# Weight products of layer 2's attention computed beside the Mamba scans of layer 0 and kept in DRAM

## The chip, the cores and the metric

The kernel runs on one core of one Trainium2 chip. The metric is the time of one execution on the device, in microseconds (us); the lower, the better. All tensors are 32-bit floats except where a name says otherwise. Engines are named as the profile names them: PE (matmuls; PEld its weight loads), DVE (vector), ACT (scalar), POOL (GpSimd), SP (here it only issues DMAs).

## The reference, cut to what matters

An image of 2 x 256 x 48 x 48 goes through four layers: layer 0 is a bidirectional Mamba block, layer 1 a linear attention with a convolution and an MLP, layer 2 a "split attention" and a mixture of experts with graph routing, layer 3 an attention with sigmoid and a second mixture of experts. The change concerns layer 2's attention, with three heads on tokens `x` (2304 per image, 256 channels):

```python
def head(W, b):                       # W: 768 x 256, b: 768
    e = einsum('bmc,hc->bmh', x, W) + b
    q, k, v = split(e, 3, axis=1)     # by thirds of the TOKENS, not of the features
    attn = softmax(einsum('bmd,bnd->bmn', q, k) * 256**-0.5)
    return einsum('bmn,bnd->bmd', attn, v)
outs = vmap(head)(W_embed, b_embed)   # three heads
out = einsum('bmd,cd->bmc', concat(outs, axis=1), W_out) + b_out + x
```

Since all three thirds use one matrix `W`, the kernel never forms `e`. The scores are `x_q (WᵀW) x_kᵀ` up to terms that the softmax removes, and the value path is `attn x_v (Wᵀ W_outᵀ)`. So the kernel needs, for each head, the 256 x 512 matrix `Wᵀ [W | W_outᵀ]`, called `gm`, and two vectors of 256, `Wᵀb` and `W_out b + b_out`, called `ub`. Both depend on weights alone.

Layer 0's scan is the recurrence `h = exp(dt·A) h + (dt·u) B`, `y = Σ_n h_n C_n`, for 512 channels, 16 states `n`, 2304 positions, 2 images and 2 directions.

## The kernel before

**Layer 0** (`layer0`) cuts a sequence into 6 chunks of `W = 384` positions. `order` lists 24 scans: image 0 forward (0 to 5), image 0 backward (6 to 11), image 1 forward (12 to 17), image 1 backward (18 to 23). One call of `scan` goes over 4 blocks of 128 channels in two pairs and 16 states in groups of 4. In a group, SP loads `bb` and `cc` (rows of B and C spread over the partitions, 768 KB each) into double buffers, POOL makes `db` (L332), and for each state ACT computes the exponential `hs` into a PSUM bank (L346), DVE runs the recurrence (L352 forward, L355 backward), DVE or POOL multiplies by C into `hc` (L360, five buffers), and PE adds `hc` into the PSUM tile `yp` by an identity matmul (L363).

Other work is woven into a scan as generators: after every second state, `slot` (1 to 32 in a scan) goes up and each entry of `beside` advances in proportion to its numbers (steps, slots by which they are to be done). These entries are `project_out` of the scan before (2 steps, only after a backward scan), `prepare` of the next scan (15 steps), and `project_in` of a later chunk (12 steps; scans 0 to 9 have one, scans 10 to 23 none). All three take their PSUM tile from `hold()`, which during the scans is the pool `ps` with the tag "mm": one bank, one buffer. The eight banks are five for `hs`, one for "mm", two for `yp`. `project_in` has ten such tiles, `prepare` nine, `project_out` two. ACT reads most of them out; DVE reads out both of `project_out` (L314) and the first of `project_in`.

The order on each engine's queue is set when the program is built, by a scheduler that starts from the order of the code and lets work that it reckons ready go first. The profile shows this: at the start of layer 2, DVE instructions of `sort_rest` (L862 to L881) and of `normalize_piece` (L95 to L105) alternate.

**Layer 1 to layer 2.** The last MLP chunk of layer 1 ends with L617 to L625 (DVE), and the last `normalize_piece` (PE L95 and L101, DVE L96, L104, L105, ACT L98, L103) makes the last 384 columns of the normalized tokens `xn`. Then `sort_rest` sorts what was left of the edge lists, on DVE. `layer2_attn` begins with the weight products: for each head, two DMAs bring `w_eo` (W_embed of the head and W_outT, 768 KB each, L675 and L676, two buffers), PE makes `gm` in two pieces of 512 columns over 6 blocks of rows (L680) and the columns of `ub` (L688), and DVE copies them out (L684, L692, L693). Then the attention proper runs for image 0 and image 1: transposes of `xn` (L708, copied out by DVE L709), `qq` = gm·xn (L717, ACT L721), scores (L729), softmax (DVE L734, ACT L738), and so on.

Of the kernel before, what the change touches and what calls it, by code (L numbers as in the profile page):

```python
# [5 lines left out]


# [1 line left out]

# [1 line left out]

# [20 lines left out]
W = 384  # L32
# [19 lines left out]
class Env:  # L52


    def __init__(self, ctx, tc, p):
        nc = self.nc = tc.nc
        self.tc, self.p, self.n_pools = tc, p, 0
        const = ctx.enter_context(tc.tile_pool(name="const", bufs=1))
        self.const = const
        self.dram = ctx.enter_context(tc.tile_pool(name="dram", bufs=1, space=DRAM))  # L60
        self.vec = const.tile([P, _NV], F32, name="vec")
        nc.sync.dma_start(self.vec, p["vecs"])
        self.ident = const.tile([P, P], F32, name="ident")
        make_identity(nc, self.ident)
        self.mean_c = const.tile([P, P], F32, name="mean_c")
        nc.vector.memset(self.mean_c, 1.0 / C)
        self.eps = {}
        for e in (1e-5, 1e-6):
            t = const.tile([P, 1], F32, name=f"eps{len(self.eps)}")
            nc.vector.memset(t, e)  # L70
            self.eps[e] = t
        self.xres = const.tile([P, 2, T], F32, name="xres")

    def uid(self):
        self.n_pools += 1
# [41 lines left out]
def layer0(ctx, E):  # L117
# [8 lines left out]
    nc, tc, p = E.nc, E.tc, E.p  # L126
# [22 lines left out]
    def hold():  # L149

        pool, tag = (ps, "mm") if scanning else (psh, "hs")
        return pool.tile([P, W], F32, tag=tag, name="mm")

    def project_in(b, c):

# [148 lines left out]
    def project_out(b, c, y):  # L304

        for m in range(2):
# [7 lines left out]
            nc.vector.tensor_tensor(xr, xr, po, ALU.add)  # L314
            yield

    def scan(step, beside, b, s, c, xs, y, dt, dtu, bcd):

        fwd = s == "f"
        yp = [None] * DB  # L320
        if not fwd:
            yf = up.tile([P, DB, W], F32, tag="ln", name="yf")
            nc.sync.dma_start(yf, yf_d[b][:, c])
        slot, done = 0, [0] * len(beside)
        for d0, g in [(d0, g) for d0 in range(0, DB, 2) for g in range(NS // GN)]:
            bb = wp.tile([P, GN, W], F32, tag="bb", name="bb")
            nc.sync.dma_start(bb, bcd[16 + g * GN : 16 + (g + 1) * GN, :].partition_broadcast(P))
            cc = wp.tile([P, GN, W], F32, tag="cc", name="cc")
            nc.sync.dma_start(cc, bcd[32 + g * GN : 32 + (g + 1) * GN, :].partition_broadcast(P))
            for d in (d0, d0 + 1):  # L330
                db = wp.tile([P, GN, W], F32, tag="db", name="db")
                nc.gpsimd.tensor_tensor(db, bc(dtu[:, d, :], [P, GN, W], 1), bb, ALU.mult)  # L332
                if g == 0:
                    yp[d] = psy.tile([P, W], F32, tag=f"y{d % 2}", name=f"yp{d}")
                    nc.tensor.matmul(
                        yp[d], lhsT=w_d[s][:, d, :], rhs=xs[:, d, :], start=True, stop=False
                    )
                    if not fwd:
                        nc.tensor.matmul(
                            yp[d], lhsT=E.ident, rhs=yf[:, d, :], start=False, stop=False  # L340
                        )
                for j in range(GN):
                    n = g * GN + j
                    on_pool = j in GP[(g + d) % 2]
                    hs = psh.tile([P, W], F32, tag="hs", name="hs")
                    nc.scalar.activation(  # L346
                        hs, dt[:, d, :], AF.Exp, scale=nega[s][:, d * NS + n : d * NS + n + 1]
                    )
                    to = wp.tile([P, W], F32, tag="ho", name="ho") if on_pool else hs
                    init = 0.0 if step == 0 else state[:, d, n : n + 1]  # L350
                    if fwd:
                        nc.vector.tensor_tensor_scan(to, hs, db[:, j], init, ALU.mult, ALU.add)  # L352
                        last = to[:, W - 1 : W]
                    else:
                        nc.vector.tensor_tensor_scan(  # L355
                            to[:, ::-1], hs[:, ::-1], db[:, j, ::-1], init, ALU.mult, ALU.add
                        )
                        last = to[:, 0:1]
                    hc = wp.tile([P, W], F32, tag="hc", name="hc", bufs=5)
                    (nc.gpsimd if on_pool else nc.vector).tensor_tensor(hc, to, cc[:, j, :], ALU.mult)  # L360
                    if step < NCH - 1:
# [12 lines left out]
        if fwd:  # L374
            nc.sync.dma_start(yf_d[b][:, c], y)
        for steps, _, _ in beside:
            for _ in steps:
                pass
# [10 lines left out]
    scanning = True  # L389
    pieces = [(0, c) for c in range(2, NCH)] + [(1, c) for c in range(NCH)]  # L390
    after = None
    for i, (b, s, step, c) in enumerate(order):
        now, ready = ready, []
        beside = [(after, 2, 5)] if after else []
        if i + 1 < len(order):
            nb, s2, _, c2 = order[i + 1]
            beside.append((prepare(nb, s2, c2, ready), 15, 25))
        if i < len(pieces):
            beside.append((project_in(*pieces[i]), 12, 32))
        scan(step, beside, *now)  # L400
        after = project_out(b, c, now[4]) if s == "b" else None
    for _ in after:
# [251 lines left out]
def layer2_attn(ctx, E):  # L654

    nc, tc, p = E.nc, E.tc, E.p
    NH, D = 3, 768  # L660
    S = L // NH
    DT, ST, HW2 = D // P, S // P, S // 2
    scale = C**-0.5
    big = ctx.enter_context(tc.tile_pool(name="l2big", bufs=1))
    xn = E.xn
    gm = big.tile([P, NH, 2, 2 * C], F32, name="gm")
    ub = big.tile([P, NH, 4], F32, name="ub")
    with (
        tc.tile_pool(name="l2wt", bufs=2) as wts,
        tc.tile_pool(name="l2wps", bufs=2, space=PSUM) as ps,  # L670
    ):
        for h in range(NH):

            w_eo = wts.tile([P, DT, 2 * C], F32, tag="w_eo", name="w_eo")
            nc.sync.dma_start(w_eo[:, :, 0:C], p["W_embed"][h].rearrange("(k p) m -> p k m", p=P))  # L675
            nc.sync.dma_start(w_eo[:, :, C:], p["W_outT"].rearrange("(k p) m -> p k m", p=P))  # L676
            for m in range(2):
                pg = ps.tile([P, 2 * C], F32, tag="pg", name="pg")
                for k in range(DT):
                    nc.tensor.matmul(  # L680
                        pg, lhsT=w_eo[:, k, m * P : (m + 1) * P], rhs=w_eo[:, k, :],
                        start=k == 0, stop=k == DT - 1,
                    )
                nc.vector.tensor_copy(gm[:, h, m, :], pg)  # L684
            pu = ps.tile([P, 4], F32, tag="pu", name="pu")
            for m in range(4):
                for k in range(DT):
                    nc.tensor.matmul(  # L688
                        pu[:, m : m + 1], lhsT=w_eo[:, k, m * P : (m + 1) * P],
                        rhs=E.v("b_embed", h * DT + k, 1), start=k == 0, stop=k == DT - 1,  # L690
                    )
            nc.vector.tensor_copy(ub[:, h, 0:2], pu[:, 0:2])  # L692
            nc.vector.tensor_tensor(ub[:, h, 2:4], pu[:, 2:4], E.v("b_out"), ALU.add)  # L693

    act = ctx.enter_context(tc.tile_pool(name="l2act", bufs=2))
    wp = ctx.enter_context(tc.tile_pool(name="l2w", bufs=2))
# [4 lines left out]
    for b in range(NB):  # L701
        t0 = b * L
        xv = act.tile([P, ST, C], F32, tag="xv", name="xv", bufs=1)
        for t in range(ST):
            o = t0 + 2 * S + t * P
# [4 lines left out]
        for h in range(NH):  # L710
            qq = act.tile([P, 2, S], F32, tag="qq", name="qq")
            for m in range(2):
                for g in range(2):
                    gs = slice(g * HW2, (g + 1) * HW2)
                    pq = ps.tile([P, HW2], F32, tag="mm", name="pq")
                    for k in range(2):
# [1 line left out]
                            pq, lhsT=gm[:, h, k, m * P : (m + 1) * P],  # L718
                            rhs=xn[:, k, t0 + g * HW2 : t0 + (g + 1) * HW2], start=k == 0, stop=k == 1,
                        )  # L720
                    nc.scalar.activation(qq[:, m, gs], pq, AF.Identity, bias=ub[:, h, m : m + 1])  # L721

            pT = act.tile([P, ST, S], F32, tag="pT", name="pT", bufs=1)
            for t in range(ST):
# [39 lines left out]
            for m in range(2):  # L764
                for g in range(2):
                    o = t0 + h * S + g * HW2
                    py = ps.tile([P, HW2], F32, tag="mm", name="py")
                    for k in range(2):
# [3 lines left out]
                        )  # L772
                    y = wp.tile([P, HW2], F32, tag="y", name="y")
                    nc.vector.scalar_tensor_tensor(
                        y, py, ub[:, h, 2 + m : 3 + m], xn[:, m, o : o + HW2], ALU.add, ALU.add
                    )
                    xr = E.xres[:, m, o : o + HW2]
                    nc.gpsimd.tensor_tensor(xr, xr, y, ALU.add)
# [1087 lines left out]
```

## Time and profile before

| | us |
|---|---|
| median of 3 runs | 5647.52 (5646.13 to 5651.45) |
| the profiled execution, whole | 5647.58 |
| its span, first to last instruction | 5645.4 |
| PE busy | 4877.7 (86%) |
| DVE busy | 3527.2 (62%) |
| POOL busy | 2398.8 (42%) |
| ACT busy | 2368.0 (42%) |
| scans of layer 0, first to last L352/L355 | 111.7 to about 2494 |
| weight products of layer 2 on PE | 3220.9 to 3275.0 |

The whole execution is 2.2 us longer than the span. The page also cuts the span into 40 slices of about 141 us with each engine's busy share. A group of instructions is given as "line, engine, operation, out<-in, shapes, count | busy us, mean ns of one | idle time before them and what ended it". A PE matmul of 32-bit floats shows as two records, so a count of 72 is 36 matmuls of the code.

### The profile page before, as it was taken

Reading aid. Unit: us, or ns where it says so; the run is one execution under the profiler, and the core shown is the slowest. Engines: PE = TensorE matmul, PEld = TensorE weight load, DVE = VectorE, ACT = ScalarE, POOL = GpSimd, SP = SyncE. Lnnn points to the kernel's source line nnn. Section 1 sums busy time; section 2 is a strip of 40 time slices with the busy share of each in tenths; the row PEclk is TensorE's granted clock in tenths of the full one; section 3 lists DMA queues with packets and bytes.
Section 4 is the critical chain, followed back from the end, with each engine's and each line's share of the span. In section 5 each row is a group of like instructions: output and inputs, shape, how many; then the busy total and the mean of one; then the engine's idle time right before and its main releaser. Section 6 shows DMA issues by size and latency. Waiting matters only on the chain. (4 is left out here: it accounts for less than half of the span.)

```text
span 5645.4 us, 47582 instructions
## 1 busy us (share of the span) xinstructions
PE 4877.7 (86%) x15480; PEld 2694.9 (48%) x15480; DVE 3527.2 (62%) x5198; ACT 2368.0 (42%) x4880; POOL 2398.8 (42%) x1295
## 2 busy tenths in 40 slices
PE   7888788877777778779999999999799999997996
PEld 3444343433333333335555555566455455554664
DVE  4899978888999988899993224456524311212333
ACT  5777666655676666622222223322033222221220
POOL 3887877777898887750000000058212100000212
PEclk9999999999999899989999999999899999998997
DMA  4444444433434444330100100111011100000323
GB/s 157 162 170 165 169 148 157 148 141 135 164 150 166 159 154 149 140 128 31 41 30 2 34 5 1 42 34 27 8 57 45 45 6 9 6 9 13 87 75 78
DMA packets 173648, 486.59 MB, mean 86 GB/s; under 512 B 31488, under 2 KB 96517, under 8 KB 173125
## 3 DMA queue, kind: packets, MB, share of 16 engines
q1 hardware_dynamic: 165252, 471.82, 23.5%
q0 software_dynamic: 8128, 11.55, 1.6%
q8 instruction: 126, 2.06, 0.1%
q14 instruction: 142, 1.16, 0.1%
HBM read 416.44 MB, written 66.86 MB: 86 GB/s over the span
## 5 line engine op out<-in xcount | busy, mean ns | idle before, releaser
L363 PE MATMUL yp<-hc,ident 128*128 128x384 f32 x3072 | 1234.5, 529 | 388.8 <-POOL hc L360 295.3
L332 POOL TENSOR_TENSOR db<-dtu,bb 128x1536 f32<-128x1536 f32 x384 | 1332.2, 3470 | 153.7 <-DVE ho L355 55.1
L363 PEld LDWEIGHTS yp<-hc,ident 128*128 128x128 f32 x3072 | 579.0, 200 | 980.8 <-POOL hc L360 454.0
L360 POOL TENSOR_TENSOR hc<-ho,cc 128x384 f32<-128x384 f32 x576 | 587.6, 1029 | 153.8 <-PE yp L363 90.7
L360 DVE TENSOR_TENSOR hc<-hs,cc 128x384 f32<-128x384 f32 x960 | 498.8, 537 | 51.0 <-PE yp L363 48.8
L346 ACT ACTIVATE hs<-dt,negab 128x384 f32<-128x384 f32 x768 | 436.2, 581 | 98.6 <-DVE ho L355 54.9
L346 ACT ACTIVATE hs<-dt,negaf 128x384 f32<-128x384 f32 x768 | 433.8, 581 | 59.2 <-DVE ho L352 28.6
L355 DVE TENSOR_TENSOR_SCAN hs<-hs,state,db 128x384 f32<-128x384 f32 x400 | 393.4, 1006 | 29.3 <-ACT hs L346 20.0
L352 DVE TENSOR_TENSOR_SCAN hs<-hs,state,db 128x384 f32<-128x384 f32 x400 | 394.9, 1006 | 20.0 <-POOL db L332 14.2
L1691 POOL DMA_INDIRECT xe<-xt_d,token x48 | 49.0, 1020 | 779.9 <-issue 768.5
L1623 PE MATMUL po<-at,xtok 128*128 128x384 f32 x864 | 334.1, 508 | 7.9 <-ACT at L1621 7.9
L252 PE MATMUL mm<-xw,w_cv 128*128 128x384 f32 x768 | 290.5, 512 | 52.9 <-DVE xres L314 18.8
L879 POOL PARTITION_ALL_REDUCE most<-most x1 | 0.4, 380 | 743.9 <-DVE ub L693 743.9
L1616 PE MATMUL sp<-qT,xn 128*128 128x384 f32 x864 | 312.1, 486 | 0.0
L1320 PE MATMUL ph<-xn,w 128*128 128x384 f32 x768 | 283.0, 510 | 23.1 <-issue 7.2
L1621 ACT ACTIVATE at<-sp 128x384 f32<-128x384 f32 x216 | 104.6, 490 | 466.1 <-PE sp L1616 463.3
L355 DVE TENSOR_TENSOR_SCAN ho<-hs,state,db 128x384 f32<-128x384 f32 x240 | 239.7, 999 | 61.8 <-POOL hc L360 52.3
L1629 DVE TENSOR_TENSOR xres<-xres,po 128x384 f32<-128x384 f32 x24 | 13.3, 554 | 410.8 <-PE po L1623 409.8
L612 PE MATMUL po<-hid,wfc 128*128 128x384 f32 x768 | 256.8, 488 | 0.0
L594 PE MATMUL pf<-t,wfc 128*128 128x384 f32 x768 | 255.3, 489 | 0.0
L352 DVE TENSOR_TENSOR_SCAN ho<-hs,state,db 128x384 f32<-128x384 f32 x240 | 238.5, 994 | 8.4 <-ACT hs L346 4.4
L1324 ACT ACTIVATE hid<-ph,vec 128x384 f32<-128x384 f32 x192 | 111.1, 580 | 301.2 <-PE ph L1320 243.6
(423 smaller groups left out, 8203.8 us busy)
## 6 DMA issues: line engine op xcount, KB each, us to landing
bb<-bcd SPq DMA_DIRECT2D x192, 768.0 KB
cc<-bcd SPq DMA_DIRECT2D x192, 768.0 KB
xw<-xi_d SPq DMA_DIRECT2D x24, 774.0 KB
w<-in_m_w SPq DMA_DIRECT2D x16, 1024.0 KB
y_d<-y SPq DMA_DIRECT2D x32, 384.0 KB
ye<-y_d SPq DMA_DIRECT2D x32, 384.0 KB
xi_d<-xz SPq DMA_DIRECT2D x48, 192.0 KB
z_d<-xz SPq DMA_DIRECT2D x48, 192.0 KB
```

The costliest lines, as they stand in the source:

```text
L252: nc.tensor.matmul(px, lhsT=w_cv[b, s][:, d * 4 + k, :], rhs=xw[:, d, o : o + W], start=k == 0, stop=k == 3,)
L332: nc.gpsimd.tensor_tensor(db, bc(dtu[:, d, :], [P, GN, W], 1), bb, ALU.mult)
L346: nc.scalar.activation(hs, dt[:, d, :], AF.Exp, scale=nega[s][:, d * NS + n : d * NS + n + 1])
L352: nc.vector.tensor_tensor_scan(to, hs, db[:, j], init, ALU.mult, ALU.add)
L355: nc.vector.tensor_tensor_scan(to[:, ::-1], hs[:, ::-1], db[:, j, ::-1], init, ALU.mult, ALU.add)
L360: (nc.gpsimd if on_pool else nc.vector).tensor_tensor(hc, to, cc[:, j, :], ALU.mult)
L363: nc.tensor.matmul(yp[d], lhsT=E.ident, rhs=hc, start=False, stop=n == NS - 1)
L594: nc.tensor.matmul(pf, lhsT=wfc1[:, k, f * P : (f + 1) * P], rhs=t1[:, k, :], start=k == 0, stop=k == 1,)
L612: nc.tensor.matmul(po[m], lhsT=wfc2[:, f, m * P : (m + 1) * P], rhs=hid[:, i, :], start=f == 0, stop=f == 15,)
L1320: nc.tensor.matmul(ph, lhsT=w1[:, e, k, f * P : (f + 1) * P], rhs=xn[:, k, c * W : (c + 1) * W], start=k == 0, stop=k == 1,)
L1616: nc.tensor.matmul(sp, lhsT=xn[:, k, t0 + i * P : t0 + (i + 1) * P], rhs=qT[:, k, c * W : (c + 1) * W], start=k == 0, stop=k == 1,)
L1623: nc.tensor.matmul(po[m], lhsT=xtok[:, i, m * P : (m + 1) * P], rhs=at, start=i == 0, stop=i == MT - 1,)
```

## The change

Layer 2's block of weight products is taken out. A generator `head_products` in `layer0` computes the same numbers in 12 steps of three yields (head `h`, half `m` of the 256 rows, half `z` of the 768 rows summed over), one step in each of the scans 10 to 21. In a step, six DMAs load three blocks of `w_eo` (a block is 128 rows of 256 floats from W_embed and as many from W_outT, 128 KB each) into the buffers of the tags "pos", "h" and "sq", which `project_in` no longer needs; three matmuls of 512 columns go into a "mm" tile, six matmuls of one column into another. For `z == 0` ACT copies the first tile into `part` and DVE the second into `E.ub`; for `z == 1` DVE adds to both, and `part` is stored in the DRAM tile `gm_d`. `E.ub` stays on the chip; `gm` is loaded in layer 2 by three DMAs of 512 KB. `hold()` and `hs` ask for 512 columns and use 384 of them.

```diff
+        self.gm_d = self.dram.tile([3, 2, P, 2 * C], F32, name="gm_d")
+        self.ub = const.tile([P, 3, 2, 2], F32, name="ub")
...
         pool, tag = (ps, "mm") if scanning else (psh, "hs")
-        return pool.tile([P, W], F32, tag=tag, name="mm")
+        return pool.tile([P, 512], F32, tag=tag, name="mm")[:, :W]
...
+    def head_products():
+        DT, D = 6, 768
+        for h, m, z in [(h, m, z) for h in range(3) for m in range(2) for z in range(2)]:
+            w_eo = []
+            for k in range(3):
+                rows = slice((z * 3 + k) * P, (z * 3 + k + 1) * P)
+                t = up.tile([P, 2, W], F32, tag=("pos", "h", "sq")[k], name="w_eo")
+                t = t.rearrange("p k w -> p (k w)")[:, : 2 * C]
+                nc.sync.dma_start(t[:, 0:C], p["W_embed"][h, rows, :])
+                nc.sync.dma_start(t[:, C:], p["W_outT"][rows, :])
+                w_eo.append(t)
+            yield
+            pg = ps.tile([P, 2 * C], F32, tag="mm", name="pg")
+            for k in range(3):
+                nc.tensor.matmul(
+                    pg, lhsT=w_eo[k][:, m * P : (m + 1) * P], rhs=w_eo[k], start=k == 0, stop=k == 2
+                )
+            if z == 0:
+                part = up.tile([P, 2 * C], F32, tag="part", name="part")
+                nc.scalar.copy(part, pg)
+            else:
+                nc.vector.tensor_tensor(part, part, pg, ALU.add)
+                nc.sync.dma_start(E.gm_d[h, m], part)
+            yield
+            pu = ps.tile([P, 2 * C], F32, tag="mm", name="pu")
+            for i in range(2):
+                o = i * C + m * P
+                for k in range(3):
+                    nc.tensor.matmul(
+                        pu[:, i : i + 1], lhsT=w_eo[k][:, o : o + P],
+                        rhs=E.v("b_embed", h * DT + z * 3 + k, 1), start=k == 0, stop=k == 2,
+                    )
+            ub = E.ub[:, h, m, :]
+            if z == 0:
+                nc.vector.tensor_copy(ub, pu[:, 0:2])
+            else:
+                nc.vector.tensor_tensor(ub, ub, pu[:, 0:2], ALU.add)
+                nc.vector.tensor_tensor(ub[:, 1:2], ub[:, 1:2], E.v("b_out", m, 1), ALU.add)
+            yield
...
-                    hs = psh.tile([P, W], F32, tag="hs", name="hs")
+                    hs = psh.tile([P, 512], F32, tag="hs", name="hs")[:, :W]
...
+    heads = head_products()
     for i, (b, s, step, c) in enumerate(order):
...
         if i < len(pieces):
             beside.append((project_in(*pieces[i]), 12, 32))
+        elif i < len(pieces) + 12:
+            beside.append((islice(heads, 3), 3, 32))
...
     gm = big.tile([P, NH, 2, 2 * C], F32, name="gm")
-    ub = big.tile([P, NH, 4], F32, name="ub")
-    with (
-        tc.tile_pool(name="l2wt", bufs=2) as wts,
-        tc.tile_pool(name="l2wps", bufs=2, space=PSUM) as ps,
-    ):
-        for h in range(NH):
...
+    ub = E.ub
+    for h in range(NH):
+        nc.sync.dma_start(gm[:, h], E.gm_d[h].rearrange("m p c -> p m c"))
```

The lines left out at the end are the loop of weight products described with the kernel before; the two readers of `ub` (L721, L774) only change their index.

More of the change, by code (lines that the diff above doesn't have):

```diff
@@ L8 @@
 from contextlib import ExitStack
+from itertools import islice
 import numpy as np
@@ L659, in layer2_attn @@
     nc, tc, p = E.nc, E.tc, E.p
-    NH, D = 3, 768
+    NH = 3
     S = L // NH
-    DT, ST, HW2 = D // P, S // P, S // 2
+    ST, HW2 = S // P, S // 2
     scale = C**-0.5
@@ L666, in layer2_attn @@
     gm = big.tile([P, NH, 2, 2 * C], F32, name="gm")
-    ub = big.tile([P, NH, 4], F32, name="ub")
-    with (
-        tc.tile_pool(name="l2wt", bufs=2) as wts,
-        tc.tile_pool(name="l2wps", bufs=2, space=PSUM) as ps,
-    ):
-        for h in range(NH):
[L674 to L693, printed above, removed]
+    ub = E.ub
+    for h in range(NH):
+        nc.sync.dma_start(gm[:, h], E.gm_d[h].rearrange("m p c -> p m c"))
     act = ctx.enter_context(tc.tile_pool(name="l2act", bufs=2))
@@ L720, in layer2_attn @@
                         )
-                    nc.scalar.activation(qq[:, m, gs], pq, AF.Identity, bias=ub[:, h, m : m + 1])
+                    nc.scalar.activation(qq[:, m, gs], pq, AF.Identity, bias=ub[:, h, m, 0:1])
             pT = act.tile([P, ST, S], F32, tag="pT", name="pT", bufs=1)
@@ L774, in layer2_attn @@
                     nc.vector.scalar_tensor_tensor(
-                        y, py, ub[:, h, 2 + m : 3 + m], xn[:, m, o : o + HW2], ALU.add, ALU.add
+                        y, py, ub[:, h, m, 1:2], xn[:, m, o : o + HW2], ALU.add, ALU.add
                     )
```

## The prediction

> **What bounds the kernel now.** I read the slices first, to see which engine is full where, then the groups and the timeline at the start of layer 2, where work is taken away, then the scans one by one, where it is put. Slices of the page, 141 us each:
>
> ```profile
> PE   7888788877777778779999999999799999997996
> DVE  4899978888999988899993224456524311212333
> ```
>
> The scans fill slices 0 to 17: DVE is at 8 to 9 tenths and PE at 7 to 8. Layer 2 begins in slice 22: PE is full, DVE is not. So the change moves PE work from a stage that PE bounds into one that DVE bounds. The groups give its size:
>
> ```profile
> L680 PE MATMUL pg<-w_eo 128*128 128x512 f32 x72 | 34.3, 635 | 0.0
> L688 PE MATMUL pu<-vec,w_eo 128*128 128x1 f32 x144 | 18.0, 258 | 3.2 <-DMA w_eo<-in_W_embed 3.2
> ```
>
> Busy 34.3 and 18.0 us, and one wait of 3.2 us for the weights. The timeline says whether anything else ran meanwhile:
>
> ```profile
> 3203.51 10.48 PE L612 MATMUL po<-hid,wfc 128*128 128x384 f32 x32
> ...
> 3216.22 1.56 PE L95 MATMUL ln_mean<-xres,mean_c 128*128 128x384 f32 x4 [2.22 <-DVE xres L625]
> ...
> 3220.93 3.35 PE L688 MATMUL pu<-vec,w_eo 128*128 128x1 f32 x22 [3.15 <-DMA w_eo<-in_W_embed]
> ...
> 3224.14 2.91 PE L101 MATMUL ln_var<-ln_sq,mean_c 128*128 128x384 f32 x4
> ...
> 3275.21 2.79 PE L708 MATMUL tp<-ident,xn 128*128 128x128 f32 x12 [0.41 <-DVE ub L693]
> ```
>
> PE goes from layer 1's last matmul (ends 3213.99) to the attention's first transpose (3275.21) in 61.2 us, without a break from 3220.9. The products lie on the path that sets the end. The scans, one window each (PE, PEld, DVE, ACT, POOL busy, then clock, DMA share, GB/s):
>
> ```profile
> 399.60:498.40 98.80, 81.87 (x226) 42.47 (x225) 89.97 (x113) 70.36 (x169) 81.95 (x42) 0.95 0.44 164
> 1358.40:1458.40 100.00, 80.18 (x217) 40.36 (x216) 81.39 (x111) 63.09 (x157) 81.21 (x42) 0.95 0.39 142
> 1548.10:1637.00 88.90, 70.06 (x185) 32.96 (x185) 86.78 (x108) 62.00 (x155) 82.44 (x42) 0.96 0.43 160
> 1909.50:2005.70 96.20, 71.69 (x178) 34.63 (x178) 84.49 (x113) 59.11 (x148) 81.89 (x43) 0.86 0.40 150
> 2109.00:2209.80 100.80, 77.74 (x210) 38.67 (x209) 86.23 (x114) 65.31 (x154) 81.34 (x42) 0.93 0.40 149
> ```
>
> These are scan 3 (forward, with `project_in`), 12 (first forward scan of image 1, with `project_out`), 14 (forward, with nothing but `prepare`), 18 (first backward, no `project_out`) and 20 (backward, with `project_out`). DVE is idle for 2.1 us of scan 14, and 9 to 19 us of the others. Scans 13 to 17 are of the tight kind, and five of the twelve new steps fall into them. Why the others are loose shows in who waited for `project_out`'s read-out on DVE (L314), us and times:
>
> ```profile
>   PEld mm L252: 23.1, 7
>   PE mm L252: 18.8, 7
> ```
>
> PE stands at the next convolution's matmul (L252) until DVE has freed the single "mm" bank, and behind it stand the `hc` matmuls.
>
> **What the Trainium skill says.** "TensorE: Matmul & The Clock Gate" (Architectural detail): PE may pull weight loads ahead of matmuls in flight, while ACT and DVE work strictly in order. So a wait at one matmul holds all behind it; the two rows above agree. "Perfetto Trace Analysis" (Optimizing Scalar/DVE Operations): an operation has a fixed overhead, on PSUM for DVE about 125 ns. The trace agrees in kind: a copy of two columns (L692) took 159 ns, so small steps are paid per instruction. "PSUM — Partial Sum Buffer" (The four PSUM rules): 512 floats fill one bank; `pg` with its 512 columns fits the "mm" bank, so the padding to 512 needs no more banks if a buffer takes a bank anyway, which no row here shows. I cost it at nothing.
>
> **The change part by part.**
>
> *Layer 2.* Of the 61.2 us, the four matmuls of L95 (1.6) and those of L101 (2.9) stay: at most 56.7 are saved, if the waits of 2.2 and 3.2 us are filled too (the transposes need only tokens of image 0, long ready). If both waits stay, 51.3. New in their place: three loads of 512 KB. The stretch that loaded the old weights moved 345 GB/s in its best slice; 1.57 MB is 4.6 us, behind which only L717 waits, not the transposes. They need nothing but room in SBUF: if that comes free when it did for L675 (3215.65), the last lands near 3221, when L717 would start. I cost them at nothing to 3 us. The cover that goes: DVE's `sort_rest` and last normalization lay beside the products. The windows 3215:3221 and 3221:3245 hold 5.8 + 11.6 us of DVE; less two copies of `gm` and one pair of `ub` (1.7), plus the six L709 (2.6): 18.3 us, so DVE is free at 3233.5 at best. PE needs its first softmax maximum at 3217.8 + 2.8 (L708) + 6.7 (L717) + 2.9 (L101) + 2.6 (first scores) = 3232.8. These are level, so a loss of 0 to 12 us if L709 stands late in DVE's queue; I take 2. **Gain 49, from 39 to 57.**
>
> *Layer 0, work.* PE gets the same 72 and 144 records: at their pace in the old block (0.43 and 0.12 us) 31 + 17 = 48 us over twelve scans, 4 each. PE is idle for 19 us in scan 14 and 23 to 25 in the backward ones: covered, except for its order. ACT gets six copies of 512 columns; L193, 384 columns, takes 478 ns, so about 0.6 each, covered by 27 us of idle time. DVE gets six additions of 512 columns, priced by L684 (0.69), and 18 of two columns (0.15): 6.9 us, 0.15 in a step with z = 0 and 1.0 in one with z = 1. Scans 13, 15 and 17 (z = 1), 14 and 16 (z = 0) have no idle DVE: 3.3 us certain there. SP gets 72 loads and six stores. L675 took 0.37 us to issue; at that price 6.5 a scan are 2.4 us, and in its waits SP stands up to 14.9 us for a `cc` buffer, so it has room. The store waits for DVE's addition, and the next group's `bb` and `cc` loads stand behind it; they have about a group's time (89/8 = 11 us) to land, and no `db` waits for a DMA today. The first six loads wait for scan 9's `project_in` to give up "h". Both: nothing, up to 1 us a scan. Data: 0.79 MB more on 14.3 (160 GB/s for 89 us), at a DMA share of 0.43: covered. POOL gets nothing; it waits more if PE frees `hc` later.
>
> *Layer 0, waits.* No row shows the two new uses of the "mm" bank, so I bound them by the two neighbours. `project_in`: scan 3 against 14 is 9.9 us, DVE 3.2 of it, so 6.7 of idleness for ten uses, 0.7 each. `project_out`: scans 19 to 22 have a mean of 101.9; scan 18, made comparable (as a first chunk its 64 recurrences take 948 instead of 1006 ns or less: some 3.4 us), 99.6; so 2.3 for two uses, DVE's 1.1 included. Upper end: scan 12 against 14, 11 us. Lower end: nothing, since `pu` comes at slot 22, after the last use by `prepare` (slot 17), and only `pg` at slot 11 stands between two of them. Less than nothing can't be excluded either where idle time is 15 us and the queue's order is redone; I give it no weight. I take 3 us for each of the five tight scans, DVE's work included, and 1.5 for the seven loose ones: 15 + 10.5 = 25.5. **Cost 25, from 7 to 76.**
>
> *Sum.* −49 + 25 = −24. Against the profiled execution's own 5647.6 us (span 5645.4 and 2.2 around it) this is 5623.6; the median of the runs is 5647.5, the same. Forecast 5623.
>
> **Rivals.** (a) *All hidden*: the new steps cost DVE's 7 us alone and layer 2 starts as if both waits stay: −51 + 7, 5603. For it: PE idle for 19 us of a tight scan, and each step's matmul block (six records of 0.43, 2.6 us) is no longer than a convolution's that runs there already. Against it: no scan with additional work has kept the tight rhythm. (b) *The tight rhythm is lost*: `pg` waiting for DVE holds PE, `hc` isn't freed, POOL stops, DVE stops; scans 13 to 17 become like scan 12 (+11 each) and the others grow by 3: 55 + 21 = 76. With the gain of 49 this is **+27, 5675, slower**. It decides from a mean cost of 60/12 = 5 us a scan. For it: scan 12 with two such uses. Against it: `project_out` comes at slots 1 and 3, just where the four convolutions want the bank, and `pg` only once among them. (c) *Layer 2 starts at DVE's pace*: all of `sort_rest` ahead of L709, PE idle from 3219 to 3233; gain 39, cost 30: 5638, no change that can be told. (d) That the products are made twice or not at all is excluded by the diff; only one writer of `gm_d` is left.
>
> **How the numbers follow.** A measurement of this kernel can tell about 0.2%, 11 us. Chances: forecast 0.42, (a) 0.26, (b) 0.16, (c) 0.16. Faster by more than 11: the forecast nearly whole (0.40), (a) whole, a quarter of (c): 0.70. Slower: (b), 0.16. The same: 0.14. The range starts at −57 + 7 = −50, just below (a), 5598, and reaches over (c) into the lower part of (b), whose cost is then some 60: 5660.
>
> **What would show it.** In the profile after: L680 and L688 gone from layer 2; from layer 1's last L612 to the first L708 some 5 to 15 us in place of 61; the `sort_rest` rows among the attention's first DVE rows; scans 10 to 21 longer by 1 to 4 us each, those with z = 1 most; new waits of PEld for the read-out of `pg`. Scans 13 to 17 at 99 us and rows "DVE ho <- POOL hc" in them would make (b) right; all at 89 to 91, (a). The forecast is wrong in its mechanism if the attention, from L708 to its end, takes a different time than before, or if scans 0 to 9 move.

## The result and the profile after

The changed kernel takes 5616.75 us (median of 4 runs, 5616.03 to 5619.78) beside 5649.49 for the kernel before: a ratio of 0.9943, interval 0.9927 to 0.9959, so faster by some 32 us. The forecast was 5623 with a range of 5598 to 5660. The profiled execution has a span of 5615.0 us, 30.4 less than before.

One correction first. The scan windows in the prediction, and the scan times in the table of the profile before, begin 11 us late, because I took the bounds from a clock that starts 11 us before the first instruction. Lengths were not touched, and of the busy times that the prediction reads in these windows scan 18's move most (PE 68.6 us in place of 71.7). From here on the bounds are the right ones (scan 14 of the kernel before is 1536.9 to 1625.8).

The slices of the page after:

```profile
PE   7887888877787877869999999998799999997996
DVE  4899978888899988899995244466524211212333
```

Layer 2 (slices 22 and 23) is as full of PE work as before; the picture at this grain hardly moves. The groups show the products in their new place, by the lines of the changed kernel (L337 was L680, L351 was L688):

```profile
L337 PE MATMUL pg<-w_eo 128*128 128x512 f32 x72 | 34.5, 595 | 1.0 <-ACT pr L276 1.0
L351 PE MATMUL pu<-vec,w_eo 128*128 128x1 f32 x144 | 16.7, 243 | 0.0
```

The same counts and nearly the same PE time; PE stands idle for 1.0 us ahead of them in all. The timeline at the start of layer 2 (start, duration, engine, line, operation, in brackets the idle time before):

```profile
3231.07 10.48 PE L661 MATMUL po<-hid,wfc 128*128 128x384 f32 x32
...
3241.39 0.82 PE L734 MATMUL tp<-ident,xn 128*128 128x128 f32 x6
...
3242.88 1.40 SPq L719 DMA_DIRECT2D gm<-gm_d  x3
...
3246.71 0.42 DVE L735 COPY xv<-tp 128x256 f32<-128x256 f32 x1
...
3249.63 5.40 PE L743 MATMUL pq<-xn,gm 128*128 128x384 f32 x16
...
3254.86 5.32 PE L755 MATMUL sp<-xn,qq 128*128 128x384 f32 x16
```

L661 (the old L612) ends at 3241.55, and the first transposes (L734, the old L708) stand directly behind it, in place of 61.2 us later. The first scores (L755, the old L729) come 13.3 us after layer 1's last matmul; before, they came 70.4 us after it (3284.36 less 3213.99), by this row of the kernel before:

```profile
3284.36 5.32 PE L729 MATMUL sp<-xn,qq 128*128 128x384 f32 x16
```

**The gain in layer 2 is 57.1 us.** The three loads of `gm` are issued at 3242.88 and nothing waits for them in these rows.

The other side, scans 14, 15 and 20, then all of scans 10 to 21, before and after (PE, PEld, DVE, ACT, POOL busy, clock, DMA share, GB/s):

```profile
1536.90:1625.80 88.90, 70.05 (x185) 32.97 (x184) 86.77 (x108) 62.00 (x155) 82.44 (x42) 0.96 0.43 161
1625.80:1714.80 89.00, 70.06 (x186) 32.92 (x185) 86.86 (x109) 62.10 (x155) 82.53 (x42) 0.96 0.43 160
2097.80:2198.70 100.90, 77.84 (x210) 38.77 (x209) 86.32 (x115) 65.41 (x154) 81.44 (x42) 0.93 0.40 149
1137.10:2300.30 1163.20, 897.99 (x2356) 436.00 (x2355) 1047.18 (x1354) 748.29 (x1714) 984.62 (x493) 0.93 0.41 151
```

```profile
1549.80:1641.80 92.00, 75.00 (x203) 36.56 (x202) 82.97 (x110) 62.31 (x156) 83.85 (x42) 0.94 0.46 164
1641.80:1736.30 94.50, 77.23 (x203) 36.88 (x202) 87.19 (x112) 62.46 (x155) 82.65 (x42) 0.93 0.46 162
2122.40:2226.70 104.30, 83.26 (x228) 42.47 (x227) 86.32 (x115) 65.93 (x155) 81.36 (x42) 0.92 0.42 152
1139.30:2331.30 1192.00, 952.33 (x2572) 475.81 (x2571) 1038.58 (x1377) 752.11 (x1720) 987.43 (x493) 0.93 0.43 156
```

The twelve scans are 28.8 us longer. PE is busy 54 us longer in them, and its idle time falls from 265 to 240 us: about half of the new PE time went into idle time, and the scans grew by the rest. DVE is not busier, although it got 7.8 us of new work, because `prepare`'s three additions now take 69.6 us in place of 87.3; its idle time rose from 116 to 153 us. All scans end 30.8 us later than before (2.4 more in scan 9, −0.4 over the other eleven outside 10 to 21).

The whole sum of the trace: +30.8 up to the end of the scans, −3.3 in layer 1, −57 at the start of layer 2, −0.9 behind it: −30.4. Layer 1 was not changed in the code. It takes 727.3 to 730.7 us in the fourteen traces of this case, and the two compared here are near the two ends of that range; single scans that no edit touches differ by 1.5 us or so, scan 9 by 2.4. I read nothing from such differences.

### The profile page after: what moved, and what is told of

It is laid out like the page before. It is cut to its first block, busy times and chain, and to the rows that moved or that the text cites. A ratio compares the mean times of both kernels' runs of the same rounds, so it can differ in the third digit from the quotient of the medians.

```text
span 5615.0 us, 47707 instructions
## 1 busy us (share of the span) xinstructions
PE 4878.6 (87%) x15480; PEld 2698.6 (48%) x15480; DVE 3511.4 (63%) x5210; ACT 2373.2 (42%) x4886; POOL 2401.8 (43%) x1295
## 5 line engine op out<-in xcount | busy, mean ns | idle before, releaser
L392 ACT ACTIVATE hs<-dt,negab 128x384 f32<-128x384 f32 x768 | 436.8, 581 | 102.5 <-DVE ho L401 57.1
L392 ACT ACTIVATE hs<-dt,negaf 128x384 f32<-128x384 f32 x768 | 434.2, 581 | 61.2 <-DVE hc L406 29.6
L256 PE MATMUL mm<-xw,w_cv 128*128 128x384 f32 x768 | 294.9, 521 | 54.9 <-DVE xres L318 18.2
L1655 DVE TENSOR_TENSOR xres<-xres,po 128x384 f32<-128x384 f32 x24 | 13.3, 555 | 411.0 <-PE po L1649 410.0
L661 PE MATMUL po<-hid,wfc 128*128 128x384 f32 x768 | 255.2, 486 | 0.0
L408 ACT COPY state<-hs 128x1 f32<-128x1 f32 x800 | 119.6, 155 | 287.8 <-DVE hc L406 286.2
```

What stands on the lines that cost most here:

```text
L256: nc.tensor.matmul(px, lhsT=w_cv[b, s][:, d * 4 + k, :], rhs=xw[:, d, o : o + W], start=k == 0, stop=k == 3,)
L392: nc.scalar.activation(hs, dt[:, d, :], AF.Exp, scale=nega[s][:, d * NS + n : d * NS + n + 1])
L661: nc.tensor.matmul(po[m], lhsT=wfc2[:, f, m * P : (m + 1) * P], rhs=hid[:, i, :], start=f == 0, stop=f == 15,)
```

## The experiments

All runs beside the kernel before on the same chip. "Stretch" is the length of scans 10 to 23 in the profiled execution, by the first recurrence of scan 10 and the end of the last: 1346.3 us before, 1374.9 in the changed kernel, so a cost of 28.6. Each stretch is read from one execution. Two pairs of kernels with the same code there agree to 0.4 us (the kernel before and the first run below; the changed kernel and the second), while the rest of the program varies by up to 13 us between the traces. So the stretch tells the runs apart better than the whole time does; differences of a few us between two stretches are still not read.

**The two halves apart.** First the gain without the cost: no steps beside the scans, and `gm_d` filled with rows of a weight.

```diff
-    heads = head_products()
+    nc.vector.memset(E.ub, 0.0)
+    for h in range(3):
+        for m in range(2):
+            nc.sync.dma_start(E.gm_d[h, m], p["W_embed"][h, m * C : (m + 1) * C, :].rearrange("(q t) c -> q (t c)", t=2))
...
-        elif i < len(pieces) + 12:
-            beside.append((islice(heads, 3), 3, 32))
```

> Nothing is computed beside the scans; gm_d is filled once with plain rows of W_embed and ub with zeros, so layer 2 starts as in the changed kernel but on other numbers (the weight products are left out altogether). Theory (gain in layer 2 is the 57 us seen in the trace, the cost lies wholly in scans 10 to 21): 5647 - 57 = 5590, give or take 4, scans 0 to 23 as before to 1 us each. Rival (part of the 57 us is paid back later in layer 2 or 3, or the scans owe some of the loss to the changed tiles of 512 columns): 5597 or more.

Measured 5590.45 beside 5646.61 (0.9901, interval 0.9884 to 0.9917): −56 us, and a stretch of 1346.6. The tiles of 512 columns cost nothing, and nothing of the 57 us is given back.

Then the cost without the gain: `layer2_attn` keeps its own products.

```diff
-    ub = E.ub
-    for h in range(NH):
-        nc.sync.dma_start(gm[:, h], E.gm_d[h].rearrange("m p c -> p m c"))
+    ub = big.tile([P, NH, 4], F32, name="ub")
+    with (
+        tc.tile_pool(name="l2wt", bufs=2) as wts,
...
```

> The steps beside the scans run as in the changed kernel, but layer 2 makes its own products again as before and does not use theirs. Theory (cost and gain are separate sums): 5647 + 31 = 5678, scans 10 to 21 longer by 2 to 3 us each, z = 0 and z = 1 alike. Rival (the cost is shared with layer 2 or layer 1 through the schedule): 5665 or less, or 5690 or more.

Measured 5681.61 beside 5646.61 (1.0061, 1.0044 to 1.0078): +35; stretch cost 28.4. The halves are separate sums; −56 and +35 add up to −21 with the intervals of both, about ±13, and the change's own −32 lies within.

**Is it the read-out of `pu`?** In the changed kernel's trace, these are the waits ahead of the `ub` rows and the waits that they cause (from the answer on the tile `pu`):

```profile
  PE pu L351: 14.9, 5
...
  PEld mm L313: 19.4, 5
```

DVE stood for 14.9 us waiting for `pu`, and `project_out`'s matmuls (L313) for 19.4 us on the bank that `pu` held. So I took it for most of the cost. In the next run ACT reads `pu` out, and DVE adds once at the end.

```diff
+        self.ubz = const.tile([P, 2, 3, 2, 2], F32, name="ubz")
...
-            if z == 0:
-                nc.vector.tensor_copy(ub, pu[:, 0:2])
-            else:
-                nc.vector.tensor_tensor(ub, ub, pu[:, 0:2], ALU.add)
-                nc.vector.tensor_tensor(ub[:, 1:2], ub[:, 1:2], E.v("b_out", m, 1), ALU.add)
+            nc.scalar.copy(E.ubz[:, z, h, m, :], pu[:, 0:2])
...
     for _ in after:
         pass
+    nc.vector.tensor_tensor(E.ub, E.ubz[:, 0], E.ubz[:, 1], ALU.add)
...
```

> The two columns of pu are read out by ACT in each step, and DVE adds the halves and b_out once at the end of layer 0 (3 small instructions), so that DVE has no pu to wait for and pu does not hold the mm bank until DVE comes by. Theory (most of the cost is DVE standing at the ub rows, 15 us in the trace, and project_out waiting for the bank that pu holds, 19 us on PE): cost 31 falls to about 16, 5602. Rival (the cost is PE's own 48 us in the order ahead of the hc matmuls): cost 27 or more, 5613 to 5617.

Measured 5617.89 (0.9947, 0.993 to 0.9963), stretch cost 35.4. DVE's wait for `pu` is gone, and that bought nothing. The other wait is not gone: PE now stands for ACT's read-out of `pu`, at `prepare`'s convolutions (L257, the L256 of the changed kernel) and at `project_out` (L314).

```profile
  PEld mm L257: 16.1, 5
...
  PEld mm L314: 12.8, 6
```

That is 28.9 us together, where the changed kernel has 22.9 (19.4 and 3.5). So this run tests half of the theory only. Next, `pu` itself is left out, and both waits with it:

```diff
-            pu = ps.tile([P, 2 * C], F32, tag="mm", name="pu")
...
-            ub = E.ub[:, h, m, :]
...
     heads = head_products()
+    nc.vector.memset(E.ub, 0.0)
```

> pu and its columns are left out (ub is zero, so the numbers of layer 2 differ). Theory (the cost lies mostly in pu's read-out and the bank that it holds): cost about 12, 5598. Rival (cost in proportion to PE time, of which pu is 17 of 48 us): cost 20, 5606. Second rival (cost lies in pg, between prepare's uses of the bank, or in the loads): cost 26 or more, 5612.

Measured 5618.44 (0.9952, 0.9936 to 0.9969), stretch cost 29.4. `pu`, with 17 us of PE time, is free, and so are both waits: the theory fell, and the second rival held.

**Loads, bank or PE time.** Three theories were left: the loads and stores in SP's queue (L), the bank (B), PE's time (P). First the steps without any matmul:

```diff
-            pg = ps.tile([P, 2 * C], F32, tag="mm", name="pg")
...
-                nc.scalar.copy(part, pg)
+                nc.scalar.copy(part, w_eo[0])
...
-                nc.vector.tensor_tensor(part, part, pg, ALU.add)
+                nc.vector.tensor_tensor(part, part, w_eo[1], ALU.add)
...
-            pu = ps.tile([P, 2 * C], F32, tag="mm", name="pu")
...
+            nc.vector.tensor_copy(E.ub[:, h, m, :], w_eo[2][:, 0:2])
```

> The loads, the store of part, one ACT or DVE read-out and a two-column copy a step stay, all matmuls of the steps and both tiles in the mm bank are left out (other numbers in layer 2). Theory L (SP's queue: the loads or the store that waits for part delay bb and cc): scans 10 to 21 still cost 25 us or more, 5614 or more. Theories P (PE's time) and B (the mm bank): cost 6 or less, 5597 or less.

Measured 5597.59 beside 5651.71 (0.9908, 0.9892 to 0.9925); stretch cost 7.2, and none of it in scans 13 to 17 (89.6, 88.9, 88.9, 93.9 and 89.4 us). I took this to clear SP's queue and DVE's additions, but the trace doesn't allow it for the tight scans. Without the matmuls the scheduler dealt the steps out earlier: all 72 loads are issued from 1055.9 to 1324.6, in scans 9 to 11, and the six additions stand in scans 10 to 12,

```profile
L339 DVE TENSOR_TENSOR part<-part,w_eo x6: 676/1627/3548, 1159.9 to 1374.2; 128x512 f32<-128x512 f32 x6
```

where the changed kernel has its own from 1301.3 to 2276.6. Scans 13 to 21 have nothing added in this run. What it shows is that all loads, stores and additions, crowded into scans 9 to 12, make these four 7.9 us longer.

Next, `pg` and `pu` are made late in each scan, after `prepare`'s last use of the bank:

```diff
                 w_eo.append(t)
-            yield
+            for _ in range(10):
+                yield
...
                 nc.sync.dma_start(E.gm_d[h, m], part)
+            yield
+            yield
             yield
...
-            beside.append((islice(heads, 3), 3, 32))
+            beside.append((islice(heads, 14), 14, 28))
```

> The same work, but pg is made at slot 21 and pu at slot 27 of 32, after prepare's last use of the mm bank (slot 17), in place of slots 11 and 22. Theory B (pg stands between prepare's uses of the one bank and pushes prepare back): cost falls from 31 to 15 or less, 5605 or less. Theory P (PE's block of 2.6 us stands ahead of hc matmuls wherever it is put): cost stays at 27 to 35, 5612 to 5622.

Measured 5621.1 beside 5651.71 (0.9944, 0.9928 to 0.9961); stretch cost 40.4, more than in the changed kernel; by the medians (−31 and −33 us) the two can't be told apart. So the cost did not fall. The run brings a bank wait of its own, though: PE stands 33.9 us at `pu` until `pg` is read out. Where the cost went is told by two windows, scans 14 and 20:

```profile
1550.30:1645.00 94.70, 76.80 (x203) 38.20 (x202) 86.01 (x110) 62.71 (x156) 81.19 (x42) 0.89 0.45 159
...
2137.10:2239.00 101.90, 82.23 (x228) 41.88 (x227) 86.37 (x116) 65.74 (x155) 81.45 (x42) 0.93 0.44 155
```

The same step costs 5.8 us in the forward scan and 1.0 in the backward one.

Next, of `pg`'s three matmuls in a step only the first is made:

```diff
             for k in range(3):
-                nc.tensor.matmul(pg, ..., start=k == 0, stop=k == 2)
+                if k == 0:
+                    nc.tensor.matmul(pg, ..., start=True, stop=True)
```

> Of the three matmuls into pg only the first is made (other numbers in layer 2): PE's block is 0.9 us in place of 2.6, while the bank is still taken and read out as before. Theory P: cost falls by more than half, to 10 to 15, 5600 to 5606. Theory B: cost stays above 25, 5612 or more.

Measured 5604.29 beside 5651.71 (0.9919, 0.9902 to 0.9935); stretch cost 16.8, a little above P's 10 to 15, and far from B's 25. Loads, stores, additions and both uses of the bank stand here in the scans where the changed kernel has them, so that all of them, with `pu` and a third of `pg`, cost no more than 16.8 us.

The waits for the bank can also be added up directly. PE's idle time just ahead of matmuls that write the "mm" bank, in scans 10 to 21, is 36.5 us before, 66.1 in the changed kernel, 45.2 in the run without `pu` and 69.9 in this one; the stretch costs are 0, 28.6, 29.4 and 16.8. The cost does not follow these waits: B, as a wait on PE, is out.

Next, the late steps again, with `pg`'s three matmuls spread over three slots:

```diff
-            yield
+            for _ in range(9):
+                yield
...
                 nc.tensor.matmul(pg, ..., start=k == 0, stop=k == 2)
+                if k < 2:
+                    yield
...
-            beside.append((islice(heads, 3), 3, 32))
+            beside.append((islice(heads, 14), 14, 28))
```

> The same work after prepare, with pg's three matmuls at slots 19, 21 and 23 and pu at 27: no block of PE longer than 0.9 us, and the bank free of prepare. Theory P (length of the block): cost 10 to 15, 5600 to 5606, clearly better than the run with pg in one block at slot 21. Theory B: like that run. Theory O (any additional instruction turns the queues' order from tight to loose): cost 25 or more in both, 5612 or more.

Measured 5618.27 (0.9942, 0.9925 to 0.9958); stretch cost 36.8, 3.6 below the run with one block, whose order of the queues it has in every scan (matched as below, 0.98 or more). So the length of PE's block is not what costs, against the reading of P that I had given it. The numbers are those of theory O, the order of the queues. The loads-alone run doesn't speak against it: in scans 12 to 21 the queues keep their order there, but nothing is added to scans 13 to 21.

Then each of `pg`'s matmuls is made twice:

```diff
             for k in range(3):
-                nc.tensor.matmul(pg, ..., start=k == 0, stop=k == 2)
+                for r in range(2):
+                    nc.tensor.matmul(pg, ..., start=k + r == 0, stop=k + r == 3)
```

> As the changed kernel, but each matmul into pg is made twice (gm comes out doubled, so layer 2's numbers differ): 31 us more of PE in scans 10 to 21. Theory P (cost grows with pg's PE time; 7, 17 and 29 us at none, a third and all of it): cost 48 to 62, 5636 to 5650. Rival (what counts is that a step is there at all and turns the order): cost below 40, 5627 or less.

Measured 5651.12 beside 5649.15 (1.0004, 0.9995 to 1.0012); stretch cost 63.3, just above what P expected, and the whole gain of the change is gone. Scans 10 to 21 with none of `pg`'s matmuls (the loads-alone run), with a third, and with all twice (the changed kernel's row is shown above):

```profile
1136.30:2306.40 1170.10, 910.15 (x2356) 441.20 (x2355) 1062.49 (x1366) 751.60 (x1719) 987.68 (x493) 0.92 0.45 158
```

```profile
1135.40:2315.90 1180.50, 931.77 (x2523) 462.91 (x2522) 1048.70 (x1377) 751.54 (x1720) 984.58 (x493) 0.93 0.44 158
```

```profile
1137.90:2365.20 1227.30, 974.01 (x2644) 485.90 (x2643) 1050.70 (x1377) 754.69 (x1720) 976.53 (x493) 0.92 0.43 152
```

At 24, 72 and 144 records of `pg`, with the loads in the same places, the stretch costs 16.8, 28.6 and 63.3 us: 0.25 us a record in the first step and 0.48 in the second, beside the 0.43 us at which the records follow one another. PE is idle for a fifth of these scans, and yet a good part of `pg` comes through.

The two steps differ, and something else changes with the records. For each engine and scan I matched the sequence of instructions in two traces, with the new ones left out; 1 means the same order. From the changed kernel to this run, every queue keeps its order (1.00) in scans 10 to 12 and 19 to 21. These six grow by 9.7 us for 36 more records, 0.27 us a record. In scans 13 to 18 DVE's order changes (0.95 down to 0.69), and the same number of records makes them 25.6 us longer, 0.71 us a record. That is more than the 0.43 us at which they follow one another, so more than `pg`'s own time is at work.

**A better place.** A late step cost backward scans 19 to 21 only 0.7 to 1.8 us each, and forward ones up to 8.5 (scan 13). The rule has an exception, scan 18, backward too, which lost 6.2. All twelve steps now go beside backward scans (`paced` takes the next part of a step at each slot named):

```diff
+    one_step, two_steps = (1, 21, 27), (1, 19, 21, 22, 27, 30)
+    plan = {10: one_step, 11: one_step, 19: two_steps, 20: two_steps, 21: two_steps, 22: two_steps, 23: two_steps}
...
+        elif i in plan:
+            beside.append((paced(plan[i]), 32, 32))
```

> The same twelve steps, all of the work, but only beside backward scans: one each in 10 and 11, two each in 19 to 23, pg and pu after slot 18. Theory (the tight forward scans 13 to 17 lose 3 to 8 us to a step because DVE has no idle time and the order of the queues changes, while a backward scan has 13 to 17 us of idle DVE and lost 1 to 2 us to a late step with its order unchanged): cost 10 to 18, 5602 to 5610, better than the change. Rival (cost is PE's time of pg wherever it stands): cost 27 or more, 5617 or more.

Measured 5611.69 beside 5649.15 (0.9934, 0.992 to 0.9947); stretch cost 21.2, above the 10 to 18 of the theory and below the 27 of its rival. That this beats the changed kernel is not shown by the times: the intervals of the two ratios overlap. Scan 14, without a step, is back at its old length, and 20 takes 5.6 us more for two steps:

```profile
1541.10:1630.00 88.90, 72.46 (x185) 34.38 (x184) 86.74 (x108) 61.90 (x155) 82.47 (x42) 0.92 0.44 160
...
2104.90:2211.40 106.50, 87.88 (x245) 45.80 (x244) 89.65 (x118) 66.26 (x155) 81.41 (x42) 0.92 0.45 159
```

Here one step cost 0 and 1.0 us (scans 10 and 11), two cost 2.9 to 6.7 (19 to 22). Scan 14 also says that PE's granted clock does not set the length of a tight scan: it takes 88.9 us at 0.92 here, and took 88.9 at 0.96 in the kernel before.

The next run moves two steps out of scan 23 (only the plan differs from the run before):

```diff
-    plan = {10: one_step, 11: one_step, 19: two_steps, 20: two_steps, 21: two_steps, 22: two_steps, 23: two_steps}
+    plan = {10: one_step, 11: one_step, 12: one_step, 18: one_step, 19: two_steps, 20: two_steps, 21: two_steps, 22: two_steps}
```

> As the run with backward scans only, but scan 23, which has no prepare beside it and only 2 us of idle DVE, gets none, and scans 12 and 18 one each. Theory: cost 12 to 20; if scan 23 suffers from two steps this is the better of the two by up to 8 us, if not it is the same to 4 us.

Measured 5619.66 beside 5649.15 (0.9948, 0.9935 to 0.9962); stretch cost 26.8, outside the 12 to 20 that were expected. In the run before, scan 23 had taken its two steps for 0.4 us; here the step beside scan 12 made scan 13, a tight one without a step, 7.2 us longer. Scan 13 in the kernel before and in this run:

```profile
1447.30:1536.90 89.60, 71.94 (x191) 34.53 (x192) 86.55 (x109) 62.30 (x155) 82.70 (x43) 0.96 0.43 159
...
1449.80:1546.60 96.80, 76.36 (x207) 38.47 (x208) 85.62 (x108) 64.10 (x158) 81.29 (x43) 0.95 0.41 147
```

No load, matmul or read-out of the products stands in it. The 16 records more on PE are `prepare`'s convolutions (L256): in the kernel before 56 of them run in scan 12 and 38 in scan 13, here 40 and 54. So a step can cost in the scan after it, by pushing work there that had run ahead. DVE's order in this scan (0.82 against the kernel before) is that of the late run (1.00 between the two), where the scan is 8.5 us longer. That run has a step in the scan too, but the 8.5 us need not come from it.

The last run gives scan 23 four steps:

```diff
+    four_steps = (1, 5, 8, 9, 13, 16, 17, 21, 24, 25, 29, 32)
+    plan = {10: one_step, 11: one_step, 19: one_step, 20: two_steps, 21: one_step, 22: two_steps, 23: four_steps}
```

> All of the work, beside backward scans only, but four of the twelve steps in scan 23 (no prepare beside it, PE busy for 58 of 81 us, and two steps there lengthened it by 0.4 us), one each in 10, 11, 19 and 21, two each in 20 and 22. Theory (a step costs 0 to 1.5 us in a backward scan that has one, 2 to 3 in one that has two, and little in scan 23): cost 12 to 18, 5602 to 5609, clearly below the changed kernel's 5617. Rival (four steps in scan 23 come through with their PE time of pg, 10 us): cost 22 or more, 5612 or more, no better than the change.

On the chip of this run both kernels took 40 us less: 5565.99 beside 5609.69 (0.9919, 0.9905 to 0.9932), −44 us. Stretch cost 22.7: scan 23 took its four steps for 4.6 us, so that the stretch is at the rival's 22 or more, above the theory's 12 to 18. Of the versions that do all of the work this is the fastest by the ratio; by the stretch it is 1.5 us behind the run with backward scans only; its interval overlaps that of the change by a hair (0.9927 to 0.9932), so that it beats the change is likely and not shown.

## Why the prediction was right, point by point

- **What bounds each stage** held. The products lay on PE's path, and their removal was worth all of it (57.1 in the trace, 56 alone).
- **The gain's size** was 49 and should have been 57, the upper end given. The term for DVE, 2 us for L709 standing late, was nearly nothing: the six copies (L735 now) are dealt in between the rows of `sort_rest` from 3246.7 on, and the first softmax maximum came 16 us after layer 1's last matmul. And I had let the two waits of 2.2 and 3.2 us stay; the transposes filled them. Rival (c), a start at DVE's pace, is thereby out. (DVE's earliest time, 3233.5, should read 3233.3 by the numbers given; nothing hangs on it.)
- **The sum** was −24 and came to some −31 in the traces. The gain was too small by 8 us and the cost by 4 to 6, and these errors cancel in part; that is luck. Layer 1's 3.3 us, which nobody forecast, make up most of the rest.
- **The cost's size** was 25 and came to 28.8 in scans 10 to 21, 30.8 with what else moved ahead of their end. The split was 15 for the five tight scans and 10.5 for the seven others; measured 12.8 and 16.0.
- **The cost's reason** was in good part wrong, and the near size is luck here too. I had counted PE's 48 us as covered by PE's idle time, and put the cost on the waits for the "mm" bank and on 3.3 us of DVE work "certain" in the tight scans. The bank waits don't account for it: without `pu` they fall from 66.1 to 45.2 us, and the cost stays. What I called covered pays, by the doses of `pg`: 0.27 us a record where the order of the queues is held. And one term got no weight: a step redoes the order of the queues and displaces other work. The prediction names the new order as a possible gain only; in the run with a step beside scan 12 it cost scan 13 7.2 us. Whether the 3.3 us of DVE work count is not shown, since the loads-alone run has its additions before scan 13. The two neighbours (`project_in`, `project_out`) from which I took the number bring matmuls, and may displace work, too; so the size came out near for other reasons than the one given.
- **The sign to be read in single scans** was wrong: steps with z = 1 should have cost most. The six with z = 0 cost 14.8 us together, the six with z = 1 14.1.
- **The wait shown for `project_out`'s read-out** (L314) hardly changed (L318 now, 22.5 us where it was 23.1).
- **Rival (b)**, the tight rhythm lost, did not come, at 2.6 us a tight scan; the late run shows it nearly (scans 13 to 16 at 94.6 to 98.1).
- **Rival (a)**, all hidden, did not come: the cost is four times DVE's 7 us.
- **The order of matmuls.** The Trainium skill ("TensorE: Matmul & The Clock Gate", Architectural detail) gives strict order to ACT and DVE, and lets PE pull weight loads ahead; that the matmuls themselves stay in program order stands further down on the same page ("Step-by-step: what each phase is for"). The trace of the kernel before agrees: at each of the seven waits of L252, three finished `hc` stood unread, and PE took them only after L252 had run. The prediction applied this to PE's wait for a bank, and not to a matmul that works. A working `pg` should hold up the `hc` matmuls behind it just as a waiting one does, but as an account of the cost this fits the backward scans and not the tight ones. DVE's waits for a `hc` that PE had not yet read, in scans 13 to 17 and then 19 to 21 of the changed kernel (us, times, longest):

```profile
DVE hc L406 <- PE yp L409: 0.4, 1, 0.4
...
DVE hc L406 <- PE yp L409: 12.9, 10, 3.0
```

In the kernel before, these were nothing in scans 13 to 17 and 8.3 us in 19 to 21. POOL's waits of this kind in scans 13 to 17 even fall, from 12.6 us to nothing.

**What stays open.** The cost has at least two parts, `pg`'s time on PE and what a step does to the order of the queues, and their shares aren't settled. DVE's order against the kernel before does not tell the cost by itself: in the changed kernel scan 15 keeps it (0.99) and is 5.6 us longer, while scan 17 loses it (0.74) and is 0.3 us shorter. With the order of all four engines held (0.98 or more, as in the late run's scans 19 to 21, PE's 18 new records left out), a step costs 0.7 to 1.8 us; in the same scans of the changed kernel, where DVE's is 0.89, 0.3 to 3.5. No run adds `pg` to a tight scan and keeps the order of all engines there, and none has the loads and the additions alone in one. Whether the one "mm" bank sets the new order, since its users take turns, was not tested. Nor is it known why `pu`, of half `pg`'s PE time, costs nothing: the run without it keeps the order of the changed kernel on every engine (0.98 to 1.00).

## What to carry to other kernels

Moving constant work out of a stage that its engine bounds was worth nearly all of the time it took there, waits included (57 of 61 us); count the waits as filled if the next work doesn't depend on what was late. In the stage that receives it, an engine's idle share was no measure of room: PE was idle for 265 of 1163 us, and 54 us more of PE time made the twelve scans 28.8 us longer. Until a run says otherwise, price such work at half of its time or more. Look at the stages next to it too, since the step may push work there that had run ahead.

When a wait is visible and plausible as the cause, take it away once before believing it, and look in the new trace whether it is gone: here one run removed only one of two waits, and the run without `pu` showed that both, 15 and 19 us, were worth nothing. When a part of the work is left out, look where the rest has gone: the loads, freed of their matmuls, had left the scans in which they were to be tested.

## What was not expected of the hardware

In the loads-alone run the six additions of 512 columns, which read SBUF there, took 10.6 us, from 0.68 to 3.55 each; the six that read `pg` from PSUM in the changed kernel took 4.1 us. They stand beside other work, and the reason was not looked for. Also, on one of the chips both kernels took 40 us less than on the others. The one trace from that chip, of the last run, has the whole difference between the first expert activation of layer 2 and the first sigmoid of layer 3: 846 us there, 884 to 891 in all other traces. Why is open.
